# A transposed copy of adj from the launch, the differences of sorted values in several steps, and the first sort woven into the first dilation

## The chip, the core and the metric

The kernel runs on one core of one Trainium2 chip. The metric is the device time of one execution in microseconds (us). Before the change three runs gave a median of 9486.65 us (9484.64 to 9487.55). All rows of instructions below come from one more execution that the hardware profiler recorded.

## The reference, cut to what matters

Input are 16 graphs of N = 1024 nodes with C = 64 channels in `x`, a 0/1 matrix `adj` of 16 x 1024 x 1024 in f32, a node mask and small weights. Four graph layers follow each other, each with a residual and a layer norm:

```python
adj_d = _dilate_adj(adj, mask)                    # drops some neighbours, both ways
agg = _weighted_nanquantile_agg(x, adj_d > 0)     # layer 0: per node and channel,
    # quantiles 0.25, 0.5, 0.75 of the neighbours' values, weighted, interpolated
...
agg = jnp.einsum('bji,bjd->bid', adj, hw) + b[l]  # layer 1, three times: adj transposed
...
deg = jnp.sum(A, axis=1)                          # layer 2: column sums of adj
message = jnp.einsum('bij,bjc->bic', A, X) * inv_deg
...
num = jnp.einsum('bij,bjd->bid', A, nodes)        # layer 3, A = edges + eye
denom = jnp.sum(A, axis=2, keepdims=True)
```

[...] So layer 1 streams rows of `adj` as they lie in memory, and layers 2 and 3 stream rows of its transpose.

## The kernel before, in words

**Layer 0 is nearly all of the time.** Each channel is sorted once over all nodes. A quantile of a node is then found by counting neighbours: TensorE multiplies the dilated adjacency `vt` with words `xw` that encode the sorted order in blocks, VectorE (DVE) compares the counts with the wanted rank, and small products turn the comparison into a block, a place in it, and a value. The work is cut into 16 graphs x 8 groups of channels x 2 halves of the nodes = 256 units (`units`), each of S = 6 slots (three quantiles, lower and upper value). Ninety-six slots are a graph. A slot `y` has two places. In each slot the main loop issues, in a fixed order written out by hand, `words`, `ranks`, `steps` of earlier slots and `masks` of the next one (class `Unit`). `masks` is the DVE pair `mt` (compare) and `pr` (multiply); `steps` multiplies `mt` with `txw`, which holds second differences of the sorted values, so that the product sums up to the wanted value. `counts` (the `x<-vt,xw` matmuls) for the unit after runs in between, and `word_part` (`pa<-words_by,prow`) makes the next words.

**The queue of each engine is in program order.** `link` chains every PE instruction to the one before it, and the class `Ordered` does the same for DVE and ScalarE (ACT) from where `Ordered.on` is set, which is the main loop; ahead of it the scheduler is free. So in the profile all DVE and ACT work of the loop carries line 337, all transposes 315, all other matmuls 318: one has to go by the tiles' names.

**Background.** Work that isn't a slot's is a generator in the list `background`, wrapped in `Spread(gen, steps, first, end, wait)`. At each place `at` runs as many of its steps as are due. `late` says how many places it lies behind an even pace. A step is put off while it is less than `wait` (LATE = 4) places late and `Ordered.through`, the planner's own estimate of when DVE gets through its queue, is over BUSY ahead of the place. At the last place everything left is run. Steps marked `"p"` need the single PSUM bank of the pool `ps_l`; no two such owners run at a time. The background of a graph g is:

- `sort_of`: the sort of the next pair of graphs. 55 stages forward on f32 (`sv`, with the comparison `m` stored in DRAM as `swaps`), then the inverse permutation backward in f16 (`sr`).
- `dilate(g + 1)`: eight blocks of 128 rows (`da` loaded, `sc` scanned on DVE, `vt`), then pairs of transposes `pq`, then the ranks `rd` and weights `wd`, which go through DRAM into `rB` and `w96`.
- `transposed(g)`: line 859. Sixteen halves of columns of `adj` are loaded as `ac` (512 bytes at a time), each turned by four f32 transposes of 128 x 128 into the bank `pt`, copied by ACT into `at` with the degrees as its accumulator, and stored in DRAM as `atd`. `ac` and `at` have one buffer each. Its `wait` is 0.
- `layers(g - 1)`: layers 0 (the end of it) to 3. `along` streams `adj` rows (layer 1) or `atd` rows (layers 2 and 3).

`info(g + 1)` isn't background: at slot 84 of a graph it calls `steps_of`, which loads the sorted values twice (`xc`, lines 514 and 515), and issues nine DVE instructions that make `txw`, all in one place.

**The head.** Ahead of the loop the program issues constants, the loads of all weights (lines 266 to 282, on SyncE's queue, SP), the mask, `rows<-onerow`, then the first sort, the first dilation, `info(0)`, `load_rank`, the words of the first group, six places of the second, the counts of unit 0 and a part of unit 1. The tail after the last slot is `layers(15)` alone, with `adj` and `atd` held in SBUF (`held`).

Of the kernel before, what the change touches and what calls it, by code (L numbers as in the profile page):

```python
# [20 lines left out]
P = 128  # L21
# [7 lines left out]
S = 6  # L29
# [8 lines left out]
def gnn_stack(  # L38
# [3 lines left out]
    xT: bass.AP,  # L42
    adj: bass.AP,
    maskT: bass.AP,
    mask: bass.AP,
# [210 lines left out]


    w1 = const.tile([P, 2, H], F32, name="w1")
    gw = const.tile([P, L, 2, C], F32, name="gw")
    wn = const.tile([P, 2, C], F32, name="wn")  # L260
    ws = const.tile([P, 2, C], F32, name="ws")
    for a in (w1, gw, wn, ws):
        V.memset(a, 0.0)
    for h in range(2):
        hp = slice(h * C, (h + 1) * C)
        nc.sync.dma_start(out=w1[hp, h], in_=W1)
        nc.sync.dma_start(out=gw[hp, :, h], in_=gW.rearrange("l d e -> d l e"))
        nc.sync.dma_start(out=wn[hp, h], in_=Wn)
        nc.sync.dma_start(out=ws[hp, h], in_=Ws)
    w2 = const.tile([H, C], F32, name="w2")  # L270
    nc.sync.dma_start(out=w2, in_=W2)

    vcol = const.tile([P, 3 + 3 * L], F32, name="vcol")
    nc.sync.dma_start(out=vcol[:, 0:1], in_=b1.unsqueeze(1))
    for h in range(2):
        hp = slice(h * C, (h + 1) * C)
        nc.sync.dma_start(out=vcol[hp, 1:2], in_=b2.unsqueeze(1))
        nc.sync.dma_start(out=vcol[hp, 2:3], in_=bias[0].unsqueeze(1))
        for i, a in enumerate((gb, gamma, beta)):
            for l in range(L):  # L280
                o = 3 + i * L + l
                nc.sync.dma_start(out=vcol[hp, o : o + 1], in_=a[l].unsqueeze(1))

    def vec(i):
        return vcol[:, i : i + 1]


    center = const.tile([P, P], F32, name="center")
    V.tensor_copy(center, ident)
    for h in range(2):  # L290
        b_ = center[h * C : (h + 1) * C, h * C : (h + 1) * C]
        V.tensor_scalar(b_, b_, -1.0 / C, None, ALU.add)

    mask8 = const.tile([P, B, T], U8, name="mask8")
# [3 lines left out]
    rows_in = [dram1.tile([5, C, N], F16, name=f"rows{i}") for i in range(2 * TURN)]  # L298
    onerow = strm.tile([P, N], F32, tag="a", name="onerow").bitcast(F16)[0:C, 0:N]
    V.memset(onerow, 1.0)  # L300
    for r in rows_in:
        nc.sync.dma_start(out=r[4], in_=onerow)

# [198 lines left out]

    def steps_of(xs, back):

        least = small.tile([P, 2], F32, tag="least", name="least", bufs=3)
        for h in range(2):
            nc.sync.dma_start(out=least[h * C : (h + 1) * C], in_=back)  # L510
        xc = dil.tile([P, 2 * N], F16, tag="d", name="xc").bitcast(F32)
        cur = xc[:, 0:512].rearrange("p (q f) -> p q f", f=F)
        prev = xc[:, 512:1024].rearrange("p (q f) -> p q f", f=F)
        nc.sync.dma_start(out=cur, in_=xs.rearrange("q p f -> p q f"))
        nc.sync.dma_start(out=prev[2:P], in_=xs[:, 0 : P - 2, :].rearrange("q p f -> p q f"))
        V.tensor_copy(prev[0:2], cur[0:2, :, 0:1].to_broadcast([2, C // 2, F]))
        V.tensor_tensor(cur, cur, prev, ALU.subtract)

        tx = prev
        V.tensor_tensor(tx[:, :, 0 : F - 1], cur[:, :, 1:F], cur[:, :, 0 : F - 1], ALU.subtract)  # L520
        V.tensor_copy(tx[:, :, F - 1 : F], cur[:, :, 0:1])
        txw = graph.tile([P, C // 2, 2, 2, F], F16, tag="txw", name="txw", bufs=2)
        part = xc[:, 0:256].bitcast(F16).rearrange("p (q f) -> p q f", f=F)
        for i in range(2):
            V.tensor_copy(part, tx)
            V.tensor_scalar(txw[:, :, i, 0, :], part, PEVEN, None, ALU.mult)
            V.tensor_scalar(txw[:, :, i, 1, :], part, PODD, None, ALU.mult)
            if i < 1:
                V.tensor_tensor(tx, tx, part, ALU.subtract)
        return txw, least  # L530

# [331 lines left out]

    def transposed(g, deg, atd):

        def half_of(i):
            ac = strm.tile([P, T // 2, P], F32, tag="ac", name="ac", bufs=1)
            j, h = divmod(i, 2)
            nc.sync.dma_start(
                out=ac, in_=adj[g, ts(h, HALF), ts(j, P)].rearrange("(t p) j -> p t j", p=P)  # L870
            )
            return ac

        ac = half_of(0)
        for i in range(2 * T):
            yield PE
            j, h = divmod(i, 2)
            pt = bank(ps_l, "pt")
            for t in range(T // 2):
                transpose(pt[:, ts(t, P)], ac[:, t, :], ident)  # L880
            at = strm.tile([P, HALF], F32, tag="at", name="at", bufs=1)
            A.activation(at, pt, AF.Copy, accum_out=deg[:, h, j : j + 1])
            nc.sync.dma_start(out=atd[j][:, ts(h, HALF)], in_=at)
            if i + 1 < 2 * T:
                ac = half_of(i + 1)

    def held(g, atd):

# [15 lines left out]
        for j in range(2 * T):  # L904
            nc.sync.dma_start(
                out=tiles[j], in_=adj[g, ts(j, P), :] if j < T else atd[j - T]
            )
        return tiles[0:T], tiles[T : 2 * T]

    def layers(g, aggd, atd, least, den, deg, rows=(), columns=()):  # L910

# [72 lines left out]
        halves_in(iv, lambda h: inv[0, ts(h, HALF)].partition_broadcast(C))  # L984
        pm = yield from along(x2, lambda j: atd[j], columns)
        msg = wide("msg", tag="hT")
# [13 lines left out]
        halves_in(iv, lambda h: inv[1, ts(h, HALF)].partition_broadcast(C))  # L1000
        pa = yield from along(x3, lambda j: atd[j], columns)
        y = wide("y", tag="yT")
# [19 lines left out]
    def all_of(gen):  # L1022
        for _ in gen:
            pass
# [72 lines left out]
    def info(g):  # L1097

        vt, rd, wd, den = parts.pop()
        xs, back = sorted_[g // TURN]  # L1100
        u = g % TURN
        txw, least = steps_of(xs[u], back[u * C : (u + 1) * C])
        infos[g] = dict(vt=vt, rd=rd, wd=wd, den=den, txw=txw, least=least, rB={})

# [22 lines left out]

    all_of(sort_of(0, sorted_))
    all_of(dilate(0, parts))
    info(0)  # L1130
    for s in range(S):
        load_rank(0, s)
    load_rows(rows_of(0), 0)

    words = {0: {}}
    for k in range(KC):
        words[0][k] = wts.tile([P, 2, T, P], F16, tag="xw", name="xw")
        for part in range(4):
            word_part(0, words[0][k], k, part)
            if part % 2:  # L1140
                word_end(words[0][k], part // 2)
    load_rows(rows_of(0), 1)

# [15 lines left out]

    for place in range(-6, 0):  # L1160
        words_at(place)
    live = {}
# [6 lines left out]
    _, counting = unit_of(0)  # L1169
    all_of(counting)  # L1170
    _, counting = unit_of(1)
    all_of(itertools.islice(counting, 68 // S))
    wvs, background, resident = {}, [], ()
    live[0].masks(0)
    for y in range(n_units * S + S):
# [4 lines left out]
        if running and z == 0:  # L1180
            infos[g]["aggd"] = dram.tile([C, N], F32, name="aggd")
            atd = dram.tile([T, P, N], F32, name="atd")
            deg = small.tile([P, 3, T], F32, tag="deg", name="deg")
            base = 2 * SLOTS * g
            if g == 0 and TURN < B:
                background.append(
                    Spread(sort_of(1, sorted_), 2 * n_sort + 6, 0, base + 2 * SLOTS + ROWS)
                )
            if g + 1 < B:
                background.append(Spread(dilate(g + 1, parts), 64, base, base + 168))  # L1190
            background.append(
                Spread(transposed(g, deg, atd), 2 * T + 2, base, base + 184, 0)
            )
            infos[g].update(atd=atd, deg=deg)

# [28 lines left out]
        for half in range(2):  # L1224

            if running:
# [14 lines left out]
                if z == 84 and half and g + 1 < B:  # L1241
                    info(g + 1)
            if running:
# [12 lines left out]
        if z == 1 and g == B:  # L1256
            resident = held(B - 1, infos[B - 1]["atd"])
        if z == S - 1 and g:
            m = infos.pop(g - 1)
            after = layers(  # L1260
                g - 1, m["aggd"], m["atd"], m["least"], m["den"], m["deg"], *resident
            )
            if g < B:
# [20 lines left out]
def arrays_of(inputs):  # L1284
# [6 lines left out]
        "xT": x.transpose(0, 2, 1),  # L1291
        "adj": inputs["adj"],
        "maskT": mask.view(np.uint8).reshape(b, n // P, P).transpose(2, 0, 1),
        "mask": mask.view(np.uint8),
# [18 lines left out]
```

## Time and profile before

| | |
|---|---|
| median of three runs | 9486.65 us |
| the profiled execution's own time | 9493.02 us |
| its span, first to last instruction | 9491.3 us |
| granted TensorE clock, mean | 0.992 |
| `pt<-ident,ac` transposes | 1024, median 273 ns each |
| `at<-pt` on ACT | 256, median 604 ns, and 256 accumulator reads, median 214 ns |
| `ac<-adj_dram`, `atd<-at` | 256 transfers each of 256 KB |
| all DMA | 743.53 MB, 26% of the 16 DMA engines |
| first `mt` of the loop | 335.97 us after the start |

How to read a row of a group: how often, the time in which at least one was running, the mean of one, then the idle time of the engine just before them and what ended it. Matmuls are pipelined: a 128 x 512 f16 one lasts 380 ns in the records, but five in a row take 1.24 us. So a matmul's price is the distance from its start to the next one's start, not its length. PE is matmul, PEld the load of weights, which lies beside it.

### The profile page before, as it was taken

How to read it: one execution, taken by the hardware profiler on the slowest of the kernel's cores; microseconds unless marked ns; L12 is line 12 of the kernel's file. 1: busy time of each engine (PE TensorE's matmuls, PEld its weight loads, DVE VectorE, ACT ScalarE, POOL GpSimd, SP SyncE). 2: the span in 40 equal slices, each digit the busy share in tenths (PEclk: the TensorE clock that was granted, in tenths of full speed). 3: DMA queues.
4: the chain of work that ended last, by engine and by line, in shares of the span. 5: the costliest groups of instructions: out<-in, count | busy, mean ns of one | idle time of the engine just before them, and what ended most of it. 6: DMA issues, size and time to landing. Idle time of an engine off the chain costs nothing.

```text
span 9491.3 us, 190992 instructions
## 1 busy us (share of the span) xinstructions
PE 8885.4 (94%) x79809; PEld 3866.0 (41%) x79809; DVE 8311.8 (88%) x9681; ACT 7185.6 (76%) x12465; POOL 203.6 (2%) x155
## 2 busy tenths in 40 slices
PE   0699999999999999999999999999999999999997
PEld 0344444444444444444444444444444444444442
DVE  9899989999898998989899898999989999777663
ACT  1588878778787787878778787877878788787772
POOL 0000000000000000000000000000000000000000
PEclk9999999999999999999999999999999999999998
DMA  3112222222223222232222322222222232222121
GB/s 94 47 48 49 94 86 77 82 76 91 85 84 79 83 81 80 94 86 78 80 80 89 83 83 85 80 84 78 97 83 83 75 87 78 75 72 74 47 69 60
DMA packets 728722, 743.53 MB, mean 78 GB/s; under 512 B 302832, under 2 KB 548720, under 8 KB 727856
## 3 DMA queue, kind: packets, MB, share of 16 engines
q1 hardware_dynamic: 727856, 731.31, 26.0%
q8 instruction: 625, 10.24, 0.5%
q14 instruction: 241, 1.97, 0.1%
HBM read 584.29 MB, written 146.81 MB: 77 GB/s over the span
## 4 chain that ended last, share of the span: by engine, by line
PE 73%; DVE 16%; ACT 5%; issue 3%; DMA 3%; SPq 0%; POOL 0%; POOLq 0%; DVEq 0%; ACTq 0%
PE x L318 31%; PE pw L318 10%; PE pa L318 10%; PE pv L318 8%; PE fc L318 6%; DVE pr L337 4%; DVE mt L337 3%; ACT dw L337 2%; DVE sr L337 2%; PE pt L315 2%; DVE sv L337 2%; DMA ac<-adj_dram 1%; PE p L318 1%; PE pc L318 1%; DVE vt L337 1%
## 5 line engine op out<-in xcount | busy, mean ns | idle before, releaser
L318 PE MATMUL x<-vt,xw 128*128 128x512 f16 x16384 | 3985.7, 380 | 82.2 <-ACT dw L337 66.5
L337 DVE TENSOR_TENSOR pr<-mt,dw 128x4096 f16<-128x4096 f16 x1536 | 3520.4, 2292 | 71.2 <-DVE mt L337 0.9
L337 DVE TENSOR_TENSOR mt<-cc,rB 128x2048 f16<-128x2048 f16 x1536 | 1871.8, 1219 | 776.5 <-PE pv L318 727.2
L318 PEld LDWEIGHTS <-xw 128*128 128x128 f16 x16384 | 1501.2, 98 | 1713.1 <-issue 405.7
L337 ACT ACTIVATE qq<-pw,col,icol 128x512 f16<-128x512 f32 x1536 | 1202.5, 783 | 776.9 <-PE pw L318 730.9
L337 ACT ACTIVATE xw<-pa 128x512 f16<-128x512 f32 x2048 | 1233.3, 603 | 489.8 <-PE pa L318 480.4
L337 ACT ACTIVATE dw<-x 128x512 f16<-128x512 f32 x2048 | 1114.9, 600 | 283.5 <-PE x L318 276.4
L337 ACT ACTIVATE xw<-xw 128x1024 f16<-128x1024 f16 x1024 | 1086.1, 1061 | 10.2
L318 PE MATMUL pw<-pr,red 128*32 128x512 f16 x12288 | 932.1, 380 | 33.7 <-DVE pr L337 33.4
L318 PE MATMUL pv<-mt,txw 128*32 128x512 f16 x12288 | 931.2, 379 | 0.2 <-ACT nt L337 0.2
L337 ACT ACTIVATE val<-pv 128x512 f32<-128x512 f32 x1536 | 926.1, 603 | 1.9 <-PE pv L318 1.3
L318 PEld LDWEIGHTS <-prow 128*128 128x128 f16 x8192 | 563.8, 98 | 865.2 <-issue 679.8
L318 PE MATMUL pa<-words_by,prow 128*128 128x128 f16 x8192 | 803.3, 221 | 106.3 <-DMA prow<-rows 92.9
L318 PE MATMUL fc<-val,fin 128*32 128x512 f32 x3072 | 789.9, 593 | 0.5 <-ACT val L337 0.5
L337 ACT ACTIVATE cc<-x 128x512 f16<-128x512 f32 x1024 | 610.2, 596 | 160.9 <-PE x L318 153.3
L318 PE MATMUL pw<-rB,subr 128*32 128x512 f16 x6144 | 616.6, 390 | 0.2
L337 DVE TENSOR_TENSOR sr<-sr 128x512 f16<-128x512 f16 x1336 | 599.8, 478 | 16.6
L318 PE MATMUL pv<-nt,nbig 128*32 128x512 f16 x6144 | 599.0, 379 | 0.0
L337 DVE TENSOR_TENSOR sv<-sv 128x512 f32<-128x512 f32 x880 | 566.7, 685 | 0.0
L318 PEld LDWEIGHTS <-txw 128*32 128x32 f16 x12288 | 330.2, 97 | 335.0 <-issue 2.9
L318 PEld LDWEIGHTS <-subr 128*32 128x32 f16 x6144 | 158.2, 93 | 658.6 <-issue 653.1
L318 PEld LDWEIGHTS <-red 128*32 128x32 f16 x12288 | 327.8, 96 | 210.5 <-issue 48.8
(3289 smaller groups left out, 7851.5 us busy)
## 6 DMA issues: line engine op xcount, KB each, us to landing
a<-adj_dram SPq DMA_DIRECT2D x360, 512.0 KB
a<-atd SPq DMA_DIRECT2D x240, 512.0 KB
da<-adj_dram SPq DMA_DIRECT2D x256, 256.0 KB
ac<-adj_dram SPq DMA_DIRECT2D x256, 256.0 KB
atd<-at SPq DMA_DIRECT2D x256, 256.0 KB
swaps<-m SPq DMA_DIRECT2D x440, 128.0 KB
m<-swaps SPq DMA_DIRECT2D x440, 128.0 KB
rB<-rd SPq DMA_DIRECT2D x96, 256.0 KB
```

Of the source, the lines that this page charges most:

```text
L315: link("PE", nc.tensor.transpose(out, in_, id_))
L318: link("PE", nc.tensor.matmul(*args, **kw))
L337: ins = call(*args, **kw)
```

## The change

1. **adj transposed by the launch.** The host hands in `adjT` beside `adj` (a layout, no arithmetic). Everything that read `atd` reads `adjT`. `transposed` becomes `degrees`: it loads halves of rows of `adjT` (2 KB at a time) into `ac`, and ACT runs over `ac` in place with the degrees as accumulator. Its steps need no bank any more, and its `wait` is the usual 4.
2. **Differences over several places.** `steps_of` is a generator with five yields. `info(g + 1)` makes it background of 6 steps, from the place after slot 84 to two places before the graph's end.
3. **The first sort ahead of the dilation.** In the head `Ordered.on` is set, the sort's stages are issued with one step of the dilation after every fourth, the rest of the dilation two steps with each part of the words, then the counts of unit 0, its first masks, the differences of graph 0, and only then the weights' loads, `center`, the six places of words and the part of unit 1.

```diff
-    def transposed(g, deg, atd):
+    def degrees(g, deg):
...
-                out=ac, in_=adj[g, ts(h, HALF), ts(j, P)].rearrange("(t p) j -> p t j", p=P)
-            )
+            nc.sync.dma_start(out=ac, in_=adjT[g, ts(j, P), ts(h, HALF)])
...
         for i in range(2 * T):
-            yield PE
+            yield
             j, h = divmod(i, 2)
-            pt = bank(ps_l, "pt")
-            for t in range(T // 2):
-                transpose(pt[:, ts(t, P)], ac[:, t, :], ident)
-            at = strm.tile([P, HALF], F32, tag="at", name="at", bufs=1)
-            A.activation(at, pt, AF.Copy, accum_out=deg[:, h, j : j + 1])
-            nc.sync.dma_start(out=atd[j][:, ts(h, HALF)], in_=at)
+            A.activation(ac, ac, AF.Copy, accum_out=deg[:, h, j : j + 1])
...
-        pm = yield from along(x2, lambda j: atd[j], columns)
+        pm = yield from along(x2, lambda j: adjT[g, ts(j, P), :], columns)
...
-        txw, least = steps_of(xs[u], back[u * C : (u + 1) * C])
-        infos[g] = dict(vt=vt, rd=rd, wd=wd, den=den, txw=txw, least=least, rB={})
+        return steps_of(xs[u], back[u * C : (u + 1) * C], infos[g])
...
-    all_of(sort_of(0, sorted_))
-    all_of(dilate(0, parts))
-    info(0)
-    for s in range(S):
-        load_rank(0, s)
+    Ordered.on = True
+    sorting, dilating = sort_of(0, sorted_), dilate(0, parts)
+    for i, _ in enumerate(sorting):
...
+        if i % 4 == 3:
+            next(dilating, None)
     load_rows(rows_of(0), 0)
-
+    load_rows(rows_of(0), 1)
...
         for part in range(4):
             word_part(0, words[0][k], k, part)
+            next(dilating, None)
             if part % 2:
                 word_end(words[0][k], part // 2)
-    load_rows(rows_of(0), 1)
+            next(dilating, None)
+    all_of(dilating)
+    stepping = info(0)
+    next(stepping)
+    for s in range(S):
+        load_rank(0, s)
...
     all_of(counting)
+    live[0].masks(0)
+    all_of(stepping)
...
-            background.append(
-                Spread(transposed(g, deg, atd), 2 * T + 2, base, base + 184, 0)
-            )
-            infos[g].update(atd=atd, deg=deg)
+                Spread(degrees(g, deg), 2 * T + 2, base, base + 184)
+            )
+            infos[g]["deg"] = deg
...
-                    info(g + 1)
+                    background.append(Spread(info(g + 1), 6, place + 1, base + 2 * SLOTS - 2))
```

## The prediction

> **What bounds the kernel now.** I read the page's engine shares and slices first, then the chain, then the busy time graph by graph, then the tile `ac` and the waits, and last one stretch of the timeline.
>
> ```profile
> PE 8885.4 (94%) x79809; PEld 3866.0 (41%) x79809; DVE 8311.8 (88%) x9681; ACT 7185.6 (76%) x12465; POOL 203.6 (2%) x155
> ...
> PE   0699999999999999999999999999999999999997
> ...
> DVE  9899989999898998989899898999989999777663
> ...
> PE 73%; DVE 16%; ACT 5%; issue 3%; DMA 3%; SPq 0%; POOL 0%; POOLq 0%; DVEq 0%; ACTq 0%
> PE x L318 31%; PE pw L318 10%; PE pa L318 10%; PE pv L318 8%; PE fc L318 6%; DVE pr L337 4%; DVE mt L337 3%; ACT dw L337 2%; DVE sr L337 2%; PE pt L315 2%; DVE sv L337 2%; DMA ac<-adj_dram 1%; PE p L318 1%; PE pc L318 1%; DVE vt L337 1%
> ```
>
> PE is full from the second slice to the last but one, the chain of work that ended last is PE for 73%, and two of its lines belong to what is removed: `pt` and the load of `ac`. In the head (first slice and a half) DVE is full and PE is not. The next view splits the loop into graphs of 568 us: span, then busy us and count of PE, PEld, DVE, ACT, POOL.
>
> ```profile
> 350.00:918.00 568.00, 539.93 (x5055) 234.19 (x5043) 551.65 (x625) 467.69 (x818) 0.98 (x1) 0.99 0.18 48
> 3190.00:3758.00 568.00, 553.80 (x4986) 240.78 (x4986) 514.58 (x602) 447.77 (x778) 11.94 (x7) 0.99 0.27 83
> 8302.00:8870.00 568.00, 559.01 (x5074) 243.64 (x5075) 421.18 (x385) 452.27 (x781) 12.33 (x7) 1.00 0.22 67
> ```
>
> The middle row stands for graphs 1 to 12: PE 97% busy, DVE 91%, ACT 79%. Graph 0 (first row) has no layers yet, and there DVE is the full one, 97%. Near the end the sort is gone, DVE falls to 421, and PE still rises only to 559. So PE binds in graphs 1 to 15, DVE in graph 0 and the head; and DVE's load costs PE about 559.0 - 553.8 = 5 us a graph.
>
> **adj transposed by the launch.** Removed are 1024 transposes and what waits round them.
>
> ```profile
> 1196.43 0.66 PE L315 MATMUL pt<-ident,ac 128*128 128x128 f32 x4
> 1196.92 0.39 PE L318 MATMUL pa<-words_by,prow 128*128 128x128 f16 x4
> 1197.15 1.24 PE L318 MATMUL x<-vt,xw 128*128 128x512 f16 x5
> 1200.06 0.63 PE L315 MATMUL pt<-ident,ac 128*128 128x128 f32 x4 [1.67 <-DMA ac<-adj_dram]
> ```
>
> The price of four is the way from start to start: 1196.92 - 1196.43 = 0.49 us, so 256 x 0.49 = 125 us. The Trainium skill ("TensorE: Matmul & The Clock Gate", Back-to-back issue gap) puts a sustained stream of weight load and 128-column matmul at about 81 ns a pair, which would make it only 1024 x 81 ns = 83 us. It doesn't say for which type; the row, with f32 and f32 weights, has 122 ns a pair, and I take the row. The last line shows the second cost: two halves fell close together, the single `ac` buffer was refilled only after the first was turned, and PE stood.
>
> ```profile
> PE pt L315 <- DMA ac<-adj_dram: 75.1, 41, 3.1
> PE ph L318 <- ACT at L337: 22.4, 13, 2.8
> ```
>
> 75.1 us of PE waiting for that load goes, and 22.4 us in which the layers' `ph` waited for ACT to empty the shared bank. Gross: 125 + 75.1 + 22.4 = 222.5 us, 13.9 a graph. The chain says nearly the same: 1% to 1.3% for the load, and of `pt`'s 2% the share 1024 of 1408 f32 transposes.
>
> What the new form costs. ACT's pass is kept, on SBUF instead of PSUM. The nearest row is `vt<-da`, the same operation with an accumulator from SBUF: 632 and 203 ns against 604 and 214 for `at<-pt`, so 17 ns more, 4 us in all, on an engine with 120 us free in each graph: nothing; without that cover 0.3 us a graph. ACT may now wait itself for the load of `ac`; behind it stand `qq`, `xw` and `dw`, for which PE would wait. The pace puts 10 places between two halves, 29 us, and the load lands in about 3: nothing, at worst the old 75 us again. SP loses 256 stores; a refill of `ac` still blocks SP until ACT has read it, as it did for `at`. The streams `a<-atd` become `a<-adjT_dram`, the same 240 x 512 KB: nothing. Written bytes fall by 256 x 256 KB = 67 MB, with DMA engines at 26%: nothing.
>
> What is late next: DVE. It has 515 to 522 us of work a graph, unchanged. With graphs of 568 us it idles some 48, with 556 some 36. If its 5 us of harm grow as the inverse of its idle time they become 6.7; if they reach the level of graph 0, where PE idles 568 - 539.9 = 28 against 14, they grow by 14. I take 4 a graph given back, bounds 2 and 8. Graphs 1 to 15: 15 x (13.9 - 4) = 149 us. Graph 0, DVE-bound: 3 us, bounds 0 and 14.
>
> **Differences over several places.** The nine instructions stay (about 5 us of DVE a graph); their stall goes.
>
> ```profile
> 1944.84 1.39 DVE L337 TENSOR_TENSOR xc<-xc 128x512 f32<-128x512 f32 x2 [3.67 <-DMA xc<-xs]
> ...
> 1952.67 0.62 PE L318 MATMUL pw<-pr,red 128*32 128x512 f16 x8 [1.41 <-DVE pr L337]
> ```
>
> DVE stood 3.67 us for the sorted values, then did the burst, and the next `pr` reached PE 1.41 us late. Pairs `mt`, `pr` are queued one slot ahead, which is why only 1.4 of some 9 us came through. In the built order of the change the loads are issued at one step and the first reader comes at the next, four places on; the burst's pieces lie in different slots. 15 x 1.4 = 21 us, bounds 0 and 40 (the chain has entries `xc<-xs` of about 5.4 us, most of which the mask and multiply behind them would fill).
>
> **The head.** The first `mt` stands at 335.97 us. Before it, DVE sorts and dilates until about 292 us (sorted rows leave SP at 296.2), words take ACT and PE from 303.3 to 319.7, counts PE to 334. Three gains. (a) SP issues 32 small weight loads first, 0.6 us each, so the sorted input is only issued at 24.07 and lands at 27.8, with DVE idle since about 16. In the built order it is SP's second transfer, and the sort's first instruction stands behind 66 small ones, at about 10 us; but 17 small loads and four `rows<-onerow` then lie between the first and the second store of `m` (two buffers), about 13 us, of which the rest of the constants (5 us) and the next stages cover a part; I leave 5 us. (b) The words' 16.4 us get dilation beside them. (c) The differences, 5 us of DVE, move behind the first masks. Against it: two blocks of 7.0 us, ten pairs of transposes at about 2.2 us (a bank is filled and read in turn) and the ranks, together some 41 us, now lie behind the sort, where they filled its gaps; and the six places of words (4 x 0.60 + 2 x 1.06 = 4.5 us of ACT) come behind the counts. Sum: sort and six blocks end at 10 (start) + 5 (constants) + (264 - 31) + 5 (that stall) = 253, where 264 is 292 - 28 and 31 what of DVE's work moved behind; plus 41, plus counts 14.4, plus 1 makes 309, plus 4.5. That is 22 us earlier; bounds 5 (if DVE, now bound to program order, loses its fill) and 40.
>
> The planner moves too: with `Ordered.on` in the head, `Ordered.through` enters the loop with some 260 us of head work while the place's clock starts at 0. Until it is worked off, about ten graphs at 557 us of places against some 525 of work, steps wait until they are 4 places late. In the built order the sums of DVE work by slot (priced by this trace) have smaller peaks in those graphs than before, 8.9 to 9.8 against 10.3 to 10.4 us, and those over 8 us are as many or fewer. I take nothing, bounds -20 and +20.
>
> **Sum.** 149 + 3 + 21 + 22 = 195 us. The profiled execution took 9493.0 (1.7 beside its span), so 9298; it lay 6.4 above the median, which gives about 9290.
>
> **Rivals.**
> - *All of it counts* (10%). DVE gives nothing back: 16 x 13.9 + 30 + 40 = 292, so 9195. For it: even with DVE at 421 the graph's PE row barely moved. Against it: graph 0.
> - *DVE takes over the beat* (12%). Half of the gross is lost in slots whose DVE work exceeds PE's: 15 x 6 + 0 + 5 = 95, so about 9390. For it: `mt` waits for `pv` in only 776 us of all. Against it: DVE ran at 97% in graph 0, so 520 us of work would allow 536.
> - *Slower* (3%). The planner's lead makes steps of sort, dilation and layers fall due together, and `pr` comes late as it did behind the burst: some 25 slots a graph have over 6.5 us of DVE work; if each stalls PE by 1.1 us for ten graphs, that is 275 us, 9292 + 275 = 9567. It decides above 195 us of new waits of `pw` for `pr` (33.4 us now). The built order speaks against it.
> - *Nothing* (3%). The transposes sat in holes that other waits would fill, or the build kept them. The built order has 1024 fewer; PE's 97% leaves few holes.
>
> **How the numbers follow.** The forecast has 72%, from 15 x (13.9 - 8) + 5 + 21 = 115 to 15 x (13.9 - 2) + 14 + 30 + 38 = 261: about 9370 to 9225. With the nearer part of the first rival the range is 9205 to 9365. Under 0.2% (19 us) no measurement of this kernel would tell from no change; faster by more 94%, within 3%, slower 3%.
>
> **What would show it.** Right: `pt` keeps only the layers' 384; no wait for `ac` on PE; a graph's length, 568 us now, near 557; PE still 95% or more and DVE 93% or 94% in graphs 1 to 12; no DVE idle for `xc`; first `mt` near 313 us. Wrong: ACT waiting for `ac`; `pw` waiting for `pr` by over 100 us; graphs shorter than 553; the first `mt` later than 331.

## The result and the profile after

| | before | after |
|---|---|---|
| median of four runs, us | 9485.65 (9482.19 to 9487.55) | 9363.36 (9361.04 to 9364.61) |
| span of the profiled execution, us | 9491.3 | 9359.3 |
| first `mt` of the loop, us | 334.8 | 343.6 |

The ratio is 0.9871, 95% interval 0.9854 to 0.9888. So 122 us are gone where 195 were forecast. The time lies inside the range, 1.6 us from its upper end. (The profile shows the first two `mt` of before as one row of 2.36 us from 334.83; the 335.97 given further up is the start of the second. Below, the first counts.)

The page of the changed kernel: engine shares, the slices of PE and DVE, and the chain that ended last with its lines. Helper lines have moved: 318 is now 278, 315 is 275, 337 is 297. (Every kernel below has its own line numbers; the tiles' names are the same.)

```profile
PE 8767.8 (94%) x78785; PEld 3749.0 (40%) x78785; DVE 8314.5 (89%) x9681; ACT 7189.3 (77%) x12465; POOL 232.7 (2%) x155
...
DVE  8799989999899998989899998999989999777663
...
PE 67%; DVE 20%; ACT 7%; issue 5%; DMA 1%; POOL 0%; SPq 0%; DVEq 0%; POOLq 0%; ACTq 0%
PE x L278 29%; PE pw L278 10%; PE pa L278 10%; PE pv L278 7%; DVE pr L297 5%; PE fc L278 5%; DVE mt L297 4%; DVE sv L297 2%; DVE sr L297 2%; ACT dw L297 2%; DVE vt L297 1%; DVE m L297 1%; PE pc L278 1%; ACT xw L297 1%; PE p L278 1%
```

PE has exactly 1024 instructions fewer, `pt` and the load of `ac` have left the chain, and DVE has gone from 16% of it to 20%. The first digit says something else: DVE was at 9 in the first slice and is now at 8.

The second view is the stretch of graphs 0, 5 and 14: span, then busy us and count of PE, PEld, DVE, ACT and POOL, the clock, DMA.

```profile
362.00:886.00 524.00, 493.29 (x4644) 210.47 (x4640) 513.36 (x565) 435.50 (x760) 0.98 (x1) 1.00 0.15 41
3122.00:3680.00 558.00, 545.62 (x4926) 232.85 (x4924) 514.06 (x605) 449.01 (x780) 14.90 (x7) 1.00 0.24 77
8146.00:8698.00 552.00, 544.32 (x4920) 232.60 (x4918) 421.70 (x395) 447.67 (x777) 12.33 (x7) 1.00 0.19 62
```

A graph has shrunk to 558 us at the same DVE work (514 us, as before), and PE is 98% busy in it. I then cut each trace at the first matmul of every graph's first slot (`pv<-nt,nbig`). The changed kernel minus before gives: head +12.3 us, graph 0 -6.7, graphs 1 to 15 -135 in all (9.0 each), tail -2.6; together -132, the difference of the spans. On PE a graph lost 6.9 us of work and 2.1 us of idle time (mean of graphs 1 to 14, from 552.5 and 14.4 us; work is the time in which the profile has PE busy). The idle time is the surprise, since 6.1 us of it a graph (75.1 and 22.4 us in 16 graphs) were tied to the removed transposes. The waits of PE show what took its place; columns are us in total, times, longest:

```profile
PE pa L278 <- ACT xw L297: 37.5, 52, 3.1
PE pw L278 <- DVE pr L297: 32.6, 38, 1.9
PE pc L278 <- DVE y L297: 29.1, 17, 3.1
...
PE x L278 <- ACT cc L297: 14.1, 19, 1.0
```

No line for `ac` is left. `pw` waits for `pr` as long as before (33.4). Grown are `pa` waiting for `xw` (12.7 us before), `pc` waiting for `y` (15.1 before) and `x` waiting for `cc` (1.4 before): ACT, an engine with over 100 us free in a graph, now comes late at some places, and DVE comes late with the `y` of the layer norms.

### The profile page after: what moved, and what is told of

It is laid out like the page before. It is cut to its first block, busy times and chain, and to the rows that moved or that the text cites. A ratio compares the mean times of both kernels' runs of the same rounds, so it can differ in the third digit from the quotient of the medians.

```text
span 9359.3 us, 188142 instructions
## 1 busy us (share of the span) xinstructions
PE 8767.8 (94%) x78785; PEld 3749.0 (40%) x78785; DVE 8314.5 (89%) x9681; ACT 7189.3 (77%) x12465; POOL 232.7 (2%) x155
## 4 chain that ended last, share of the span: by engine, by line
PE 67%; DVE 20%; ACT 7%; issue 5%; DMA 1%; POOL 0%; SPq 0%; DVEq 0%; POOLq 0%; ACTq 0%
PE x L278 29%; PE pw L278 10%; PE pa L278 10%; PE pv L278 7%; DVE pr L297 5%; PE fc L278 5%; DVE mt L297 4%; DVE sv L297 2%; DVE sr L297 2%; ACT dw L297 2%; DVE vt L297 1%; DVE m L297 1%; PE pc L278 1%; ACT xw L297 1%; PE p L278 1%
## 5 line engine op out<-in xcount | busy, mean ns | idle before, releaser
L297 ACT ACTIVATE xw<-xw 128x1024 f16<-128x1024 f16 x1024 | 1085.3, 1060 | 11.2
L278 PE MATMUL pw<-pr,red 128*32 128x512 f16 x12288 | 930.4, 379 | 33.1 <-DVE pr L297 32.6
L774 POOL TENSOR_TENSOR rstd<-var,neghalf 128x8 f32<-128x8 f32 x112 | 222.2, 1984 | 8112.3 <-DVE var L297 8112.3
```

What stands on the lines that cost most here:

```text
L278: link("PE", nc.tensor.matmul(*args, **kw))
L297: ins = call(*args, **kw)
L774: nc.gpsimd.tensor_tensor(rstd, var, neghalf, ALU.pow)
```

## The experiments

All ratios are to the kernel before, run beside each kernel on the same chip, with 95% intervals.

| kernel | ratio | first `mt`, us |
|---|---|---|
| changed kernel | 0.9871 [0.9854, 0.9888] | 343.6 |
| p1_adjT: transposed copy alone | 0.9829 [0.9813, 0.9846] | 336.0 |
| p2_spread: spread differences alone | 0.9998 [0.9990, 1.0007] | 335.5 |
| p3_head: new head alone | 1.0098 [1.0083, 1.0113] | 343.1 |
| p12_old_head: copy and spread | 0.9857 [0.9842, 0.9871] | 335.4 |
| p3_reset: p3_head, planner's lead set to 0 | 1.0012 [1.0005, 1.0019] | 344.8 |
| e_reset: changed kernel, lead set to 0 | 0.9873 [0.9858, 0.9888] | 344.5 |
| q_free: copy, new head, scheduler left free in it | 0.9807 [0.9792, 0.9822] | 320.4 |
| r_latew: copy, old head, weights' loads late | 0.9809 [0.9795, 0.9824] | 321.0 |
| p12_near: p12_old_head, pieces at successive places | 0.9855 [0.9840, 0.9869] | 335.1 |
| s_best: changed, free head, differences in one place | 0.9815 [0.9800, 0.9829] | 319.2 |
| h_apart: before, halves of `adj` kept apart | 1.0026 [1.0016, 1.0036] | 336.0 |
| g1_nodeg: copy alone, no degrees | 0.9815 [0.9799, 0.9832] | 335.9 |

### The three parts, one at a time

Theory: the copy gives its gain and the head takes part of it away, before or in the loop. Rival: the copy itself gives less, because DVE takes over. Each kernel below is before with the named part of the diff (in p3_head `info(0)` stands in one piece ahead of `load_rank`, since it lacks the spread).

```diff
 p1_adjT       + part 1 of the change
 p2_spread     + part 2
 p3_head       + part 3
 p12_old_head  + parts 1 and 2
```

> Before, with the transposed copy of adj alone. If the head is what the whole change lost, this alone is 16 graphs x 9 us = 145 us faster (about 9340) and its first mt stays at 336 us. If the prediction's sizes hold, 152 us (about 9335). If the planner's lead of the new head is what shortened graphs 1 to 9, less: 16 x 7.5 = 120 us (about 9365), with graphs of 559 to 560 us throughout, as graphs 11 and 12 have in the changed kernel.

> Before, with the differences over several places alone. The prediction's sum: 21 us faster (about 9465). Rival, that a freed stall only moves to the next wait of PE for ACT or DVE: 0 to 8 us.

> Before, with the new head alone, the differences of graph 0 made ahead of its first masks. The trace of the changed kernel reads as a head that is longer by 9 to 12 us: first mt at 344 to 352 us instead of 336. If the planner's lead helps nine graphs by 2 us each, the time is 5 us shorter to 5 us longer (about 9485); if it does nothing, 8 to 15 us longer (about 9497). The prediction's sum said 22 us shorter (9464).

> The changed kernel with the head of before: transposed copy and spread differences. If the new head only costs, this is 12 us faster than the changed kernel (about 9351). If its planner's lead shortens nine graphs by 2 us, it is 6 us slower (about 9369).

The copy alone takes 162 us (0.0171 of 9482.9; 146 to 177). By the traces it leaves the head as it is and takes 11.2 us from each of graphs 1 to 15. The same stretch of graph 5 in p1_adjT:

```profile
3105.00:3660.00 555.00, 545.32 (x4927) 232.82 (x4926) 514.67 (x605) 448.53 (x781) 12.52 (x7) 1.00 0.25 78
```

It has the PE work of the changed kernel and 3 us less idle time. So DVE did not take over, and the rival falls. Two waits of PE grew; first before, then p1_adjT:

```profile
PE pc L318 <- DVE y L337: 15.1, 11, 3.1
PE x L318 <- ACT cc L337: 1.4, 2, 1.0
```

```profile
PE pc L319 <- DVE y L338: 32.4, 20, 3.1
PE x L319 <- ACT cc L338: 12.7, 23, 1.3
```

The spread alone gives nothing. On top of the copy it costs 0.9857 - 0.9829 = 0.0028, 26 us; the two intervals just meet, but no run of p12_old_head is below 9348 us and none of p1_adjT above 9325. The head on top of both costs another 0.0014, 13 us; here the intervals overlap widely, and only the spans of the traces (9349.1 and 9359.3) and the first `mt` point the same way. The sum closes: 162 - 26 - 13 = 123 us. The head alone costs 93 us on before, far more than any of the three expected values. Its first `mt`, 8 us later, is the smaller part: graphs 1 to 10 are 5 to 10 us longer each, 7.6 in the mean, and from graph 11 on they are within about 2 us of before.

### Why the head lengthens ten graphs of the kernel before

Theory: the planner's lead of some 260 us, until it is worked off. Rival: something lasting that the new order leaves behind, such as where buffers or the queue of SP stand.

```diff
     wvs, background, resident = {}, [], ()
+    Ordered.through = 0
```

> Before with the new head, and the planner's estimate of DVE's queue set back to 0 ahead of the loop. If the lead of 260 us is what made graphs 1 to 10 of the new head alone 7 to 8 us longer each, they come back to 566 to 569 us and the time is 8 to 14 us above before (about 9494): the head's own cost. Rival, that the head's order itself leaves queues or buffers in a worse state: graphs stay at 574 to 577 us (about 9575).

> The changed kernel with the planner's estimate set back to 0 ahead of the loop. If the lead does harm only where the transposes compete for the one bank, nothing moves here: 9358 to 9368 us, first mt at 344, graphs of 555.5 (odd) and 560.7 (even) as with the old head. If it harms as it did on the kernel before, 60 to 80 us faster (about 9290).

With that line 82 of the 93 us are gone (1.0098 to 1.0012), so it is the lead. PE's waits in p3_head, then those in p3_reset:

```profile
PE pq L275 <- DVE x L297: 48.3, 10, 5.0
PE pt L275 <- DVE yn L297: 41.8, 22, 4.3
PE pt L275 <- DMA ac<-adj_dram: 38.5, 26, 2.8
```

```profile
PE pt L275 <- DMA ac<-adj_dram: 72.9, 41, 2.9
...
PE pt L275 <- DVE yn L297: 13.2, 4, 4.3
```

The first line has exactly 10 events of about 4.8 us: once in each of the ten graphs, near the end of the dilation, its `rw` transposes (`pq`) stand behind the one bank of `ps_l`, which the layer norm holds until DVE has read it. With the lead a step is put off until it is late, and so the owners of that bank meet; without it the line is gone.

These rows explain about half of the 82 us: 48.3 and 28.6 more, 34.4 less. Most of the rest is in the clock that the trace records. In graphs 1 to 10 it stands at half for 71.7 us in p3_head and for 20.5 us in p3_reset, in stretches of 3.4 or 6.8 us. In them the `x<-vt,xw` matmuls start every 427 ns, outside every 216, so half of the 51 us more, some 26 us, is lost. The long waits are tied to it: at the end of each of the ten waits for the bank, or within 3.4 us of it, the clock was at half. The same holds for only 6 of the 40 waits over 1 us of `pt<-ident,ac` in graphs 1 to 14 of before, of which the longest is 2.7 us.

In the changed kernel the same line does nothing (0.9873 against 0.9871). There the lead only changes which waits there are: `pa` for `xw` falls from 37.5 us to 13.8, and `pw` for `pr` rises from 32.6 to 49.4. With `transposed` gone, one of the owners of the bank is gone, and no wait of `pq` for `x` over 1.6 us is left. That the missing owner is the reason is read from the waits, not tried by itself.

### Why the head itself is later, not earlier

e_reset against p12_old_head is the head's own cost without the lead: 0.9873 - 0.9857, 15 us (the intervals overlap; of the spans' difference of 15.7 us, 12.6 lie in the head and 5.0 in graph 0); on before (p3_reset) it is 11. Theory: the fixed program order on DVE and ACT in the head. Rival: the order of the work itself, the dilation behind the sort. q_free has the copy and the same new order in the program's text, but leaves the scheduler free (and so has no lead either); r_latew leaves the old head and moves only the block of the weights' loads behind the first counts.

```diff
 q_free (on p1_adjT with part 3):
-    Ordered.on = True
 r_latew (on p1_adjT):
     all_of(counting)
+    w1 = const.tile(...)      # the block from here to `center`,
+    ...                       # taken from its place ahead of the sort
```

> The transposed copy with the new head, but the scheduler free ahead of the loop as in before, so no order of DVE and ACT by the program and no lead of the planner; differences in one place. If the fixed order is what made the head long (DVE idle behind stores, ACT's dilation behind words that wait), the first mt comes at 315 to 330 us instead of 343.6, graphs are those of the copy alone, and the time is 9300 to 9318. Rival, that sort ahead of dilation is itself the longer way: first mt at 338 to 345, 9325 to 9331.

> The transposed copy with the old head, but the loads of the weights written behind the first counts, so that the sorted input is SP's second transfer. If the late start of the sort (27.8 us) is worth what the prediction said, first mt 8 to 15 us earlier (321 to 328), time 9307 to 9315. If the small loads still get between the first stores of m, 0 to 6 us (9316 to 9322).

The first `mt` comes at 320.4 and 321.0 us, 23 us ahead of the changed kernel and 14 to 15 ahead of before. s_best, shown further down, differs from the changed kernel in the head by the line `Ordered.on = True` alone, and has 319.2. So fixing the order is what costs. It is not shown that the written order is sound: left free, the scheduler doesn't keep it. In q_free DVE starts the scans of all eight blocks of the dilation by 164.2 us, beside the sort; in the changed kernel the last two start at 289.9 and 297.6, behind it. Nor does the weave give anything of its own: the old order with late loads of the weights (r_latew) has the same first `mt`. In q_free the sort ends 14 us sooner than in r_latew (267.8 and 281.5), but the way from there to the first `mt` is 13 us longer. So the late loads are worth 15 us of the first `mt`, and nothing else in the new head a measurable amount. In the time none of these is clear of the copy alone: their intervals (0.9807 to 0.9815) overlap with its own (0.9829).

DVE's first comparison of the sort starts at 5.16 us in the changed kernel, where before it waited for an input that landed at 27.8. The timeline of the changed kernel's head (start, duration, engine, operation, in brackets the idle time before it) shows where these 22 us and more were lost. (The earlier start isn't all gain: in before DVE made constants in that time, and stood only 11.6 us for the loads.)

```profile
150.46 0.69 DVE L297 CAST sr<-ii 128x1024 f16<-128x1024 int32 x1 [9.41 <-DMA xs<-sv]
...
278.50 1.08 SPq L432 DMA_DIRECT2D rows<-sr  x2
282.12 2.94 SPq L458 DMA_DIRECT2D prow<-rows  x8
284.97 1.86 PE L278 MATMUL pa<-words_by,prow 128*128 128x128 f16 x16 [272.28 <-DMA prow<-rows]
285.59 0.60 ACT L297 ACTIVATE xw<-pa 128x512 f16<-128x512 f32 x1 [55.69 <-PE pa L278]
287.44 0.49 DVE L297 TENSOR_SCALAR vt<-vt,sk 128x1024 f16<-128x1024 f16 x1 [8.96 <-ACT vt L297]
...
343.59 1.23 DVE L297 TENSOR_TENSOR mt<-cc,rB 128x2048 f16<-128x2048 f16 x1 [15.66 <-ACT cc L297]
```

At 150.46 DVE stands 9.41 us for the stores of the sorted values, and nothing of the dilation may pass. At 287.44 it stands 8.96 us for `vt` from ACT, ACT's `vt` (it runs from 286.08) stands behind `xw`, `xw` behind `pa`, and `pa` behind a load that follows the end of the sort: a step of the dilation that needs none of these hangs at the end of the sort, because ACT's queue says so. A further 8.7 us are DVE's waits for the bank `pq`. In the first 300 us DVE is busy for 259.7 us where it was 268.6, although its sort started 22 us sooner. The sixth block of the dilation ends at 288.7; from there to 329.3 the rest of the dilation and the words follow, then 14.3 us of counts, and 343.6. In q_free the same `mt` follows a wait of 1.25 us:

```profile
320.45 2.36 DVE L298 TENSOR_TENSOR mt<-cc,rB 128x2048 f16<-128x2048 f16 x2 [1.25 <-ACT cc L298]
```

### Why spreading the differences costs

First theory: the pieces late in the graph come on top of slots that are already full, so pieces at once behind slot 84 should cost nothing. Rival: a piece costs wherever it lies outside slot 85.

```diff
-                    background.append(Spread(info(g + 1), 6, place + 1, base + 2 * SLOTS - 2))
+                    background.append(Spread(info(g + 1), 6, place + 1, place + 7, 0))     # p12_near
```

> Transposed copy and spread differences with the old head, but the six steps at successive places right after slot 84 instead of up to the graph's end. If the spread cost 26 us because its last pieces leave DVE late for the heavy first slots of the next even graph (pr late at slots 1, 2, 8, 9), even graphs fall from 560.7 to 555 to 558 us and the time to that of the copy alone, 9320 to 9330. If the pieces cost wherever they lie between other slots' work, it stays at 9340 to 9350.

> The changed kernel with the scheduler free in the head and the differences of later graphs in one place again; those of graph 0 stay behind the first masks. From the free head with the copy (first mt 320.4 us, of which DVE stood 11 us for the sorted values) the first mt comes at 308 to 318 us, graphs are those of the copy alone, the time is 9296 to 9308. If the values' load was not on the head's path, 9308 as there.

p12_near stays at 0.9855, so my first theory fell. There are two reasons. The first is that on the copy the stall had already gone. DVE's waits for the sorted values in before:

```profile
DVE xc L337 <- DMA xc<-xs: 36.9, 15, 3.7
```

In p1_adjT, with the burst still in one place, they are 0.9 us in all. SP issues the first of the two loads there some 30 us ahead of the burst, in before 5.3 to 5.7 us ahead. (That this is because SP has lost the stores of `atd` and the waits around them was not tried by itself.) So on the copy the spread had nothing to remove.

The second reason is where the pieces lie. The lead of DVE shows it: the time from the end of a slot's `pr` to the start of the first `pw` that reads it, mean of graphs 4, 6 and 8, in us. Slots 0 to 14 are those at the begin of the same graphs, to which the shortfall of the graph ahead is carried.

| slot | 85 | 86 | 88 | 92 | 95 | 0 | 4 | 8 | 10 | 14 |
|---|---|---|---|---|---|---|---|---|---|---|
| p1_adjT, one burst | 8.4 | 4.8 | 6.3 | 3.5 | 4.9 | 3.6 | 3.0 | 3.0 | 2.2 | 6.5 |
| p12_old_head | 8.4 | 7.7 | 4.9 | 3.9 | 2.7 | 0.1 | 0.1 | 0.7 | 0.1 | 7.1 |
| p12_near | 8.4 | 7.7 | 1.6 | 0.4 | 1.8 | 1.2 | 0.7 | 0.7 | 0.1 | 7.1 |
| before, one burst | 6.5 | 0.1 | 4.8 | 5.9 | 4.9 | 4.5 | 3.0 | 3.0 | 4.0 | 5.4 |
| p2_spread | 6.5 | 6.8 | 8.4 | 5.9 | 3.3 | 2.5 | 1.9 | 1.9 | 3.3 | 5.5 |

The timelines of DVE around slot 85 of graph 4, first p1_adjT, then p12_near:

```profile
3027.19 1.23 DVE L338 TENSOR_TENSOR mt<-cc,rB 128x2048 f16<-128x2048 f16 x1 [1.86 <-PE pv L319]
...
3032.69 1.39 DVE L338 TENSOR_TENSOR xc<-xc 128x512 f32<-128x512 f32 x2
...
3036.92 1.22 DVE L338 TENSOR_TENSOR mt<-cc,rB 128x2048 f16<-128x2048 f16 x1
```

```profile
3032.81 1.23 DVE L338 TENSOR_TENSOR mt<-cc,rB 128x2048 f16<-128x2048 f16 x1 [1.86 <-PE pv L319]
3039.63 1.23 DVE L338 TENSOR_TENSOR mt<-cc,rB 128x2048 f16<-128x2048 f16 x1 [1.68 <-PE pv L319]
3046.04 1.23 DVE L338 TENSOR_TENSOR mt<-cc,rB 128x2048 f16<-128x2048 f16 x1 [1.80 <-PE pv L319]
3056.13 1.22 DVE L338 TENSOR_TENSOR mt<-cc,rB 128x2048 f16<-128x2048 f16 x1
```

At slots 84 to 86 DVE is as far ahead of PE as its buffers let it: `mt` waits for `pv` to free one. In p1_adjT the burst falls into just this time. The wait of 1.86 us stands in both, but the burst, 4.7 us long, takes the place of the next two, 1.68 and 1.80 us. The lead falls from 8.4 to 4.8 us, and PE doesn't notice. In p12_near DVE stands out these waits idle, and does most of the pieces afterwards, where it has no time to spare: the lead is used up at slots 92 to 95 and in the first slots of the graph, and `pr` comes late there. Waits of `pw` for `pr` in p1_adjT, p12_old_head and p12_near:

```profile
PE pw L319 <- DVE pr L338: 34.1, 37, 4.4
```

```profile
PE pw L319 <- DVE pr L338: 48.9, 67, 2.9
```

```profile
PE pw L319 <- DVE pr L338: 47.8, 59, 2.9
```

The longest wait gets shorter (4.4 to 2.9), but there are many more of them. These lines carry some 15 of the 26 us; the rest is not tied to a row. That the held slots are what makes the burst free is read from these leads; no run put the pieces into other held slots. On before alone things are different: there the burst does use up the lead (0.1 us at slot 86), and the spread leaves 1.9 us or more in these slots. It takes 9 us of `pw`'s waits for `pr` (33.4 to 24.2), and yet none of the time; what takes the 9 us back is not tied to a row.

s_best is the version drawn from this: all of the change, with the free head and the differences of later graphs in one place. It gives 0.9815. This, q_free and r_latew can't be told apart (0.9807 to 0.9815), and each is below the changed kernel with intervals that do not meet. In its head DVE stands 11.3 us for `xc`. With the differences behind the first masks the first `mt` comes at 319.2 us, only about 1 us ahead of q_free, where 308 to 318 had been expected; so that load is hardly on the head's path.

### The wait for ac alone, and the degrees

h_apart asks what the 75 us wait is worth with the transposes kept: two halves must lie three places apart. g1_nodeg asks what ACT's pass over `ac` costs; it runs over one column, so the degrees are left out of its result.

```diff
 h_apart (on before):
-            yield PE
+            yield "3" + PE
 g1_nodeg (on p1_adjT):
-            A.activation(ac, ac, AF.Copy, accum_out=deg[:, h, j : j + 1])
+            A.activation(ac[:, 0:1], ac[:, 0:1], AF.Copy, accum_out=deg[:, h, j : j + 1])
```

> Before, where two halves of the transposition never follow each other by less than 3 places (some 8.7 us), so that the load of ac has landed; all transposes stay. If the 75 us in which PE waited for ac were on the path, 50 to 75 us faster (about 9420). Rival, that such waits only move to ACT or the next layer's step: 0 to 20 us (9463 to 9483).

> The transposed copy alone, with ACT's pass over each half of it cut to one column (the degrees are left out). The prediction took the pass as hidden: 0 to 5 us faster than the copy alone (9317 to 9322). If ACT's bunches now take the place of the waits that went (some 2 us a graph of PE waiting for cc and words after such a pass), 15 to 40 us faster (about 9295).

h_apart removed the wait and got slower, by 0.26%, which neither theory expected. Its halves slid to the end of their stretch, and the last one met the layer norm's hold on the bank, once a graph:

```profile
1986.50 0.69 DVE L337 TENSOR_TENSOR yn<-pc,rstd 128x512 f32<-128x512 f32 x1 [0.27 <-POOL rstd L810]
...
1987.30 1.09 PE L315 MATMUL pt<-ident,ac 128*128 128x128 f32 x4 [4.58 <-issue]
...
1988.60 1.91 PE L318 MATMUL x<-vt,xw 128*128 128x512 f16 x4
```

In all there are 14 such waits:

```profile
PE pt L315 <- issue: 65.6, 14, 4.8
```

The profile calls the 4.58 us "issue"; it is the bank, which `yn` reads until 1987.19, just ahead. So 75.1 us of short waits became 65.6 us of long ones, and PE's idle time in graphs 1 to 14 is nearly as before (14.6 and 14.4 us a graph). What made it slower is seen in the rows behind the wait: four transposes take 1.09 us, in before 0.66, and four `x` 1.91 us, in before five 1.24. The clock stood at half there. It did so at the end of all 14 waits, or within 3.4 us of it, and in graphs 1 to 14 for 102.4 us in all, in before for 30.7; half of the difference is 36 us, more than the 24 us that the kernel lost. The run does not say what the wait for `ac` is worth by itself.

g1_nodeg is 13 us (0.0014) faster than the copy alone, with overlapping intervals; the spans differ by 7. So ACT's pass costs at most 0.4 to 0.8 us a graph, which is not clear of nothing. In the changed kernel the pass itself is as costed:

```profile
L297 ACT ACTIVATE ac<-ac x256: 617/632/709, 410.2 to 9179.2; 128x512 f32<-128x512 f32 x128
L297 ACT ACTIVATION_READ_ACCUMULATOR ac<-ac x256: 188/202/279, 410.7 to 9179.7; 128x1 f32 x128
```

## Why the prediction was right and wrong, point by point

- **The bound.** Right. PE binds in graphs 1 to 15: it is 98% busy, and the 6.9 us of work that a graph lost came out of the span.
- **adj transposed: 152 us.** Right, 162 measured alone. PE's work fell by 7.3 us a graph (6.9 in the changed kernel) where 125 / 16 = 7.8 was forecast. That is 107 to 114 ns a pair, or 102 to 105 without the 0.7 and 0.1 us that a shorter time at half clock saved. It is below the row's 122 and above the 81 ns of the Trainium skill ("TensorE: Matmul & The Clock Gate", Back-to-back issue gap), which would have given 5.2 us. The row was a little too high: the transposes' own ways from start to start come to 7.7 us a graph, but those of `pa`, which often stands behind them, grew by 1.1 us when they were gone. Of the gross 13.9 us a graph 13.9 - 11.2 = 2.7 were given back, where I had taken 4: 0.5 of work, the rest idle time. Of that the rows name DVE's late `y` (15.1 to 32.4 us) and ACT's late `cc` (1.4 to 12.7), together 28.6 us or 1.9 a graph; DVE's `pr`, on which the argument went, stayed (33.4 to 34.1). The size was near, the place was not foreseen. "SP loses 256 stores" was taken for nothing on the way; SP then issued the loads of the sorted values far earlier, and the next term lost its reason. "ACT with 120 us free: nothing" was nearly so, by g1_nodeg.
- **Differences spread: 21 us.** Wrong: 0 alone, -26 on the copy. Two steps failed. "Their stall goes" counts a gain that the copy makes already (36.9 us of DVE's waits to 0.9 in p1_adjT). And "the nine instructions stay" (they are eleven, 4.7 us) took them for free wherever they lay; by the leads they were free in the time in which DVE is held by full buffers, and cost 1.7 us a graph of PE's time elsewhere.
- **The head: 22 us.** Wrong in sign: -13 on the other two parts. "Sort and six blocks end at 253" failed: the sort started at 5.2, even earlier than forecast, but ended at 278.5, and the sixth block at 288.7. The step "bounds 5 (if DVE, now bound to program order, loses its fill)" names the cause and gives it too small a size. It allowed for 22 - 5 = 17 us; the bound order lost 23 (343.6 against q_free's 320.4). The 41 us behind (measured 40.6) and the counts of 14.4 (14.3) were right. Of the three gains only the loads' (a) is seen, in r_latew.
- **The planner's lead: 0, bounds -20 and +20.** 0 was right for the changed kernel (e_reset), and the bounds were wrong for the mechanism: with the transposes kept it is 82 us. I argued from sums of DVE work per slot; the cost lay in the one PSUM bank and in the half clock that came with each wait for it.
- **The rivals.** "All of it counts", "DVE takes over the beat" and "nothing" fell with p1_adjT. "Slower" named the lead rightly, but by waits of `pw` for `pr`, which did not grow (32.6).
- **The signs.** As forecast: `pt` with 384 transposes, no wait for `ac` on PE or ACT, a graph of 558 (557), PE above 95%. DVE is 92%, not 93 to 94. The first `mt` at 343.6 had been named as a sign of being wrong, and was.

The parts add up: 195 + 10 (copy) - 47 (spread) - 35 (head) = 123 us. That the total still fell in the range is luck: the largest term was right, the two small ones missed by 82 us together, and the range ended 1.6 us above the time.

## What to carry to other kernels

Work on an engine that runs ahead can cost nothing in the slots where its buffers hold it back, and cost time elsewhere (here 1.7 us a graph for 4.7 us of work): before spreading a burst, look at the lead it falls into (end of the producer to start of the consumer, slot by slot), not only at the stall ahead of it. Of two parts of a change ask whether the first removes what the second is for: here the copy had already removed the stall. An early start is worth only what a fixed queue lets through: list what stands behind each wait in program order on every engine, as one instruction here tied a step to the end of the sort. And a single bank with several owners turns any shift of background work, a planner's state too, into waits of 4 to 5 us, and here each of these also came with 3.4 us or more at half clock; removing one owner can be what makes the shift harmless.

## What the runs showed of the hardware that was not expected

- Loading and turning f32 blocks of 128 x 128 on TensorE cost 122 ns a pair by the row (0.49 us for four), and 102 to 114 ns by the work that a graph lost with 64 of them.
- A wait of PE of 4.5 to 5.0 us came each time with 3.4 or 6.8 us at half clock, at its end or within 3.4 us of it (10 of 10 in p3_head, 14 of 14 in h_apart), with matmuls 427 ns apart instead of 216. Of 40 waits of 1.0 to 2.7 us in before, 6 were. So one long wait cost more than several short ones of the same sum.
- Thirty-two small loads took SP about 0.6 us each, so that it issued the sort's input at 24.07 us; with them behind the first counts (r_latew) the loop begins 15 us sooner.
- PE waits 4.5 to 5.0 us for a single PSUM bank that a layer norm holds; the profile shows this once as `pq` waiting for `x` (p3_head) and once as "issue", with no releaser at all (h_apart).
